# Attention sums queued later, taps respread, and row transfers re-timed in a metaformer layer with routed experts

## The chip, the cores and the metric

One core of a Trainium2 chip runs the whole kernel. The metric is device time in microseconds (us); the median of 3 runs is 2202.95 (2195.85 to 2204.05). All data is fp32.

## The reference, cut to what matters

Four images of 256 channels and 32 x 32 pixels (N = 1024 positions) go through one layer and then through a feed-forward with eight experts. The layer has a selective scan in four channel groups (Mamba), gated 1-D convolutions, an attention with 8 heads over the 1024 positions, a mixing product, a 3x3 convolution per channel, two normalisations and a projection; the feed-forward sends each position to its two best experts.

```
# scan, in each of four groups:
h = dA_t * h + dBu_t;  y_t = sum over states of h * C_t
# attention, 8 heads of 32:
att = softmax(q @ k.T / sqrt(hd));  o = (att @ v) @ outw.T + outb
# then, per image: mix o with the convolutions (fc), normalise, gelu,
# 3x3 convolution per channel, normalise over the image, project
# feed-forward:
gate = top 2 of softmax(x @ Wg + bg)
out += weight_e * (gelu(x @ W1[e] + b1[e]) @ W2[e] + b2[e])   for the two chosen e
```

## The kernel before, in words

The order of the work is written out by hand. Pieces of work are Python generators; `start` puts one into the list `running`, and each `beat` gives every generator in it one step, if its time has come: what a generator yields is the number of beats until its next step. The instructions go to each engine in the order in which they are emitted so, and each engine works through its own queue in that order; semaphores make an instruction wait for its data.

**The scan** is cut into 32 parts (an image, one of four groups, one half of the positions: eight parts an image) of 16 steps. A step is a decay on ACT (L715), an inflow on DVE (L725), the scan itself on DVE (L736), the product with C on Pool (`dA`, L744) and a sum over states on PE (`yp`, L754); a beat follows each step. Beside it run the work of other images: the convolutions of the image before (`g`, `d` at L454 and L459, `qd`, `gp`), normalisation, and the routing of the image before (`dispatch`, from L1779).

**The pauses.** After the fourth part of image b, for b = 1, 2 and 3, the scan pauses. Attention of image b-1 starts, with the mixing product behind it (`joined`); beside it run the end of the scan part (`finish_part`, with `op` at L769 and L773), and as one chain the `local` convolution of image b-1, `around` of image b-2 (the 3x3 convolution: L1305 to L1334), and further pieces. In the last pause, with attention of image 2, that chain ends in `taps_ahead(3)`: it loads image 3's rows (L587), scales them on ACT (L569), adds two shifted products on DVE (L576, four in all for the two channel blocks) and stores them (L581) for the last convolutions. Beats go on until attention has reached its third last step; then the scan resumes while attention ends.

**Attention** (L1101 to L1190) takes 32 key steps: two head groups, two halves of the queries, eight key blocks. Step by step it emits four logits matmuls for the next step (L1123, one for each head of the group, tile `st`) and their four exps on ACT (L1133, tile `e`), then four matmuls with v (L1169, tile `av`). The softmax's sums come from a product with ones: on odd steps DVE adds the e of two steps (L1179, four additions), and `sum_pair` (L1141 to L1145) multiplies the result by ones (L1143). In the kernel before it is emitted after the av of the next step. `end_block` divides (L1147 to L1159).

**The 3x3 convolution** in `around` (from L1319) takes eight taps besides the centre, two DVE operations each (one for each channel block); it yields 1 after each tap.

**Routing** of an image (`dispatch`) finds the two best experts of each position, counts with two matmuls how many positions before it chose the same expert (`places`, L1867 and L1868, from `oh`), works out each position's row, scales the rows, and then sends them out with 16 indirect transfers from Pool into the DRAM buffer `XS` (L1934, each after a small memset of `apart` at L1933). `follow` makes one instruction wait for another.

**The tail.** After the scan, the last convolutions run with expert tiles beside them; then tiles are held, attention of image 3 runs with its `local`, with image 2's routing under way, then the rest of image 3 and the remaining tiles. A tile loads rows (`xs` from `XS`, L2160), transposes them on PE (`xp`, L2218), and multiplies with the weights (`h`, L2259, gelu on ACT; `y`, L2272); `ys` are added into the output buffer by indirect transfers from Pool (L2299). At the end the rows come back and are added to the result (L2324 to L2331).

The emission of `sum_pair`, before:

```
for i in range(4):
    nc.tensor.matmul(accs[0][ts(i, HD)], v8[...], es[i], ...)
if pairs:
    sum_pair()
if kt % 2 == 0:
    first = es
else:
    for i in range(4):
        nc.vector.tensor_tensor(first[i], first[i], es[i], ALU.add)
    pairs.append((kt, accs[1], first))
```

Of the kernel before, what the change touches and what calls it, by code (L numbers as in the profile page):

```python
# [75 lines left out]
def network(  # L76
# [71 lines left out]
    with tc.tile_pool(name="w_conv", bufs=1) as wp, tc.tile_pool(  # L148
# [955 lines left out]
        def attention(b):  # L1104

            v8, qk = QKV.pop(b)
            rows = [  # L1110
                largest(b, g, qk[g][:, 0, :], qk[g][:, 1, :]) if shifted else None
                for g in range(2)
            ]
            yield 1
            steps = [(g, h, kt) for g in range(2) for h in range(2) for kt in range(NK)]

            def logits(g, h, kt):

                q, k = qk[g][:, 0, :], qk[g][:, 1, :]
                sts = [ps(f"st_{b}_{g}_{h}_{kt}_{i}") for i in range(4)]  # L1120
                for i in range(4):
                    r = ts(i, HD)
                    nc.tensor.matmul(  # L1123
                        sts[i], k[r, ts(kt, P)], q[r, half(h)], start=True, stop=not shifted
                    )
                    if shifted:
                        nc.tensor.matmul(
                            sts[i], ones[HD * i : HD * i + 1, :],
                            rows[g][HD * i : HD * i + 1, half(h)], start=False, stop=True,
                        )  # L1130
                es = [a2(f"e_{b}_{g}_{h}_{kt}_{i}") for i in range(4)]
                for i in range(4):
                    nc.scalar.activation(es[i], sts[i], AF.Exp, scale=1.0 / HD**0.5)  # L1133
                return es

            log_exp()
            ahead = logits(*steps[0])
            pairs, accs, ending = [], [None, None], []

            def sum_pair():  # L1140
                kt, acc, es = pairs.pop()  # L1141
                for i in range(4):
                    nc.tensor.matmul(  # L1143
                        acc[ts(i, HD)], ones[:, 0:HD], es[i], start=(kt == 1), stop=(kt == NK - 1)
                    )  # L1145

            def end_block(g, h, values, total):  # L1147

                low, out = a2(f"low_{b}_{g}_{h}"), OT[b][g][:, half(h)]
                at = (2 * b + g) * 2 + h  # L1150
                nc.scalar.activation(low, total, AF.Ln, bias=added)
                if shifted:
                    nc.scalar.activation(low, low, AF.Exp, scale=-1.0)
                else:
                    nc.vector.tensor_reduce(sums[:, 0, at : at + 1], total, AX.X, ALU.max)
                    nc.scalar.activation(
                        low, low, AF.Exp, scale=-1.0, accum_out=sums[:, 1, at : at + 1]
                    )
                nc.vector.tensor_tensor(out, values, low, ALU.mult)  # L1159

            for at, (g, h, kt) in enumerate(steps):
                es = ahead
                if at + 1 < len(steps):
                    ahead = logits(*steps[at + 1])
                if kt == 0:

                    accs = [ps(f"av_{b}_{g}_{h}_{w}") for w in range(2)]
                for i in range(4):
                    nc.tensor.matmul(  # L1169
                        accs[0][ts(i, HD)], v8[:, kt, ts(4 * g + i, HD)], es[i],  # L1170
                        start=(kt == 0), stop=(kt == NK - 1),
                    )
                if pairs:
                    sum_pair()
                if kt % 2 == 0:
                    first = es
                else:
# [3 lines that stand above are left out]
                    if ending:  # L1181
                        end_block(*ending.pop())
                if kt == NK - 1:
                    ending.append((g, h, *accs))
                if at == len(steps) - 3:
                    T["attended", b] = True
                yield 1
            sum_pair()
            yield 1
            end_block(*ending.pop())  # L1190
            yield 1
# [90 lines left out]
        def around(b):  # L1282

            xc = XC.pop(b)
            mv = small.tile([P, NC2, 2], F32, tag="mv", name=f"mv_{b}")
            for c in range(NC2):
                st = small.tile([P, 2, 6], F32, tag="bn", name=f"bn_{b}_{c}", bufs=2)
                for h in range(2):
                    nc.vector.bn_stats(st[:, h, :], xc[:, c, half(h)])
                nc.vector.bn_aggr(mv[:, c, :], st.rearrange("p a b -> p (a b)"))  # L1290
                yield 1
            rs = small.tile([P, NC2, 2], F32, tag="rs", name=f"rs_{b}")
            root(rs[:, :, 0:1], mv[:, :, 1:2], eps5)
            yield 1
            nc.vector.scalar_tensor_tensor(
                rs[:, :, 1:2], mv[:, :, 0:1], -1.0, rs[:, :, 0:1], ALU.mult, ALU.mult
            )
            yield 1
            xi = XC[b] = a8(f"xi_{b}")
            xz = [  # L1300
                act4.tile([P, HH, WW], F32, tag="a4", name=f"xz_{b}_{c}") for c in range(NC2)
            ]
            pace(b, PACE["taps"])
            for c in range(NC2):
                nc.vector.tensor_scalar(  # L1305
                    xz[c].rearrange("p i j -> p (i j)"), xc[:, c, :], rs[:, c, 0:1], rs[:, c, 1:2],
                    ALU.mult, ALU.add,
                )
            for c in range(NC2):
                nc.vector.tensor_scalar(  # L1310
                    xi[:, c, :], xz[c].rearrange("p i j -> p (i j)"), col("dwc_w", 9 * c + 4),
                    col("dwc_b", c), ALU.mult, ALU.add,
                )
            yield 1
            for k in (0, 1, 2, 3, 5, 6, 7, 8):
                (to_i, at_i), (to_j, at_j) = (edge(d - 1) for d in divmod(k, 3))
                for c in range(NC2):
                    acc = xi[:, c, :].rearrange("p (i j) -> p i j", j=WW)
                    nc.vector.scalar_tensor_tensor(  # L1319
                        acc[:, to_i, to_j], xz[c][:, at_i, at_j], col("dwc_w", 9 * c + k),  # L1320
                        acc[:, to_i, to_j], ALU.mult, ALU.add,
                    )
                yield 1

        def sent_off(b):

# [39 lines left out]
            pace(b, PACE["routing"])  # L1366
            for ticks in experts.dispatch(
                b, xr, act8.tile(experts.XR, F32, tag="a8", name=f"XR_{b}"), root,
                log_exp,
            ):  # L1370
                if experts.counted == b:
                    pace(b, PACE["rows"])
                yield ticks
# [166 lines left out]
        with tc.manual_schedule(engines=ALL):  # L1540
# [4 lines left out]
            for b in range(B):  # L1545
                for p in range(PARTS):
# [15 lines left out]
                    if b > 0 and p == PARTS // 2 - 1:  # L1562
                        drain()
                        start(
                            one_by_one(attention(b - 1), joined(b - 1)), finish_part(at),
                            one_by_one(
                                local(b - 1), *([around(b - 2)] if b > 1 else []),
                                *([normalised(b + 1)] if 1 < b < B - 1 else []),
                                *([taps_ahead(b)] if b == B - 1 and b in XD else []),
                            ),  # L1570
                        )
                        if b > 1:
                            flag = "attending" if b == B - 1 else "joining"
                            start(behind_flag((flag, b - 1), sent_off(b - 2)))
                        if b == 1:
                            start(normalised(b + 1))
                        while not T.get(("attended", b - 1)):
                            beat()
                        resume(at + 1)
# [41 lines left out]
class Experts:  # L1621
# [154 lines left out]
    def s1(self, name):  # L1776
        return self.m0.tile([P, self.NT, 1], F32, tag=name, name=name)

    def dispatch(self, b, X1, XR, root, log_exp):  # L1779

        nc, tc, psum, m0, NT = self.nc, self.tc, self.psum, self.m0, self.NT
        s1, s3, all_e = self.s1, self.s3, self.all_e
# [77 lines left out]
        nc.vector.tensor_tensor(oh, oh1, oh2, ALU.add)  # L1860
        ex, w_1 = s1("ex"), s1("w_1")
        nc.vector.tensor_tensor(ex, m_2, m_1, ALU.subtract)
        yield 1
        cp = bank(f"places_{b}")
        flat = oh.rearrange("p t e -> p (t e)")
        W = NT * NE
# [64 lines left out]
        for j in range(2):  # L1931
            for t in range(NT):
# [6 lines left out]
                for other in self.sent + self.read:  # L1939
                    tc.declare_no_dep(ins.ins, other.ins, reason="no two share a row")  # L1940
                self.sent.append(ins)
                if b == self.B - 1 and j == 0:
                    self.blank_end(t)
                yield 2 if b in (0, 2) or b == 1 and t % 2 else 1
# [487 lines left out]
```

## Time and profile before

| | |
|---|---|
| median of the runs | 2202.95 us |
| profiled execution: time / span | 2182.24 us / 2180.3 us |
| mean granted TensorE clock | 0.953 |
| PE busy | 1937.3 us (89%), 8690 matmuls |
| weight loads busy | 874.4 us (40%) |
| DVE busy | 1533.4 us (70%) |
| ACT busy | 1212.4 us (56%) |
| Pool busy | 1048.1 us (48%) |
| key steps of attention, images 0 / 1 / 2 / 3 | 437.0-537.1 / 795.5-897.5 / 1193.0-1292.6 / 1605.9-1688.5 us |
| end of the scan's last product on Pool | 1449.6 us |
| row transfers of images 0 / 1 / 2 / 3, first to last issue | 1033-1100 / 1391-1445 / 1610-1633 / 1846-1870 us |

Times of the trace count from the start of the span. A row of the groups gives line, engine and operation, the output and inputs by name, the shape, the count, then busy time, the mean of one, and the idle time just ahead of it with what ended that. A bracket in the timeline has the idle time of the engine ahead of an instruction and the instruction that released it. A stretch of the program's windows gives the busy time of each engine in it.

### The profile page before, as it was taken

Reading aid. Unit: us, or ns where it says so; the run is one execution under the profiler, and the core shown is the slowest. Engines: PE = TensorE matmul, PEld = TensorE weight load, DVE = VectorE, ACT = ScalarE, POOL = GpSimd, SP = SyncE. Lnnn points to the kernel's source line nnn. Section 1 sums busy time; section 2 is a strip of 40 time slices with the busy share of each in tenths; the row PEclk is TensorE's granted clock in tenths of the full one; section 3 lists DMA queues with packets and bytes.
Section 4 is the critical chain, followed back from the end, with each engine's and each line's share of the span. In section 5 each row is a group of like instructions: output and inputs, shape, how many; then the busy total and the mean of one; then the engine's idle time right before and its main releaser. Section 6 shows DMA issues by size and latency. Waiting matters only on the chain. (4 is left out here: it accounts for less than half of the span.)

```text
span 2180.3 us, 28168 instructions
## 1 busy us (share of the span) xinstructions
PE 1937.3 (89%) x8690; PEld 874.4 (40%) x8690; DVE 1533.4 (70%) x2231; ACT 1212.4 (56%) x2272; POOL 1048.1 (48%) x930
## 2 busy tenths in 40 slices
PE   6778778999978999987789999768999999999995
PEld 2113112322212332222123223225642668888884
DVE  4989998857999988799898888985365356121211
ACT  4665657668668577776566776625168423222221
POOL 0887887712888740476977025752040013422221
PEclk8988999999999999998999999889999999999997
DMA  3565553401444421153634024454230166967665
GB/s 107 146 162 123 127 125 91 106 22 59 116 115 107 111 60 39 34 132 100 177 79 113 1 78 101 104 177 123 78 115 1 46 196 198 261 186 191 175 162 167
DMA packets 157087, 251.40 MB, mean 115 GB/s; under 512 B 34740, under 2 KB 101332, under 8 KB 156664
## 3 DMA queue, kind: packets, MB, share of 16 engines
q1 hardware_dynamic: 136560, 223.47, 37.8%
q0 software_dynamic: 12720, 17.32, 4.0%
q10 hardware_dynamic: 7640, 8.65, 1.2%
q8 instruction: 72, 1.18, 0.2%
q14 instruction: 95, 0.78, 0.1%
HBM read 137.22 MB, written 36.62 MB: 80 GB/s over the span
## 5 line engine op out<-in xcount | busy, mean ns | idle before, releaser
L744 POOL TENSOR_TENSOR dA<-hs,cs 128x512 f32<-128x512 f32 x512 | 683.2, 1342 | 374.8 <-DVE hs L736 315.8
L715 ACT ACTIVATE dA<-dts,A 128x512 f32<-128x512 f32 x512 | 358.7, 718 | 159.2 <-DMA dts<-dt 71.8
L754 PE MATMUL yp<-dA,quads 128*32 128x512 f32 x1024 | 290.0, 640 | 85.3 <-POOL dA L744 74.0
L2299 POOL DMA_INDIRECT Y<-ys,dest x68 | 108.8, 1601 | 507.6 <-DVE ys L2291 500.2
L1133 ACT ACTIVATE e<-st 128x512 f32<-128x512 f32 x512 | 263.8, 605 | 93.2 <-PE st L1123 85.8
L2264 ACT ACTIVATE hs<-h,b 128x256 f32<-128x256 f32 (+1 forms) x256 | 110.5, 478 | 334.7 <-PE h L2259 231.7
L725 DVE TENSOR_TENSOR dBu<-dts,bs 128x512 f32<-128x512 f32 x384 | 260.0, 678 | 49.8 <-PE bs L707 14.8
L736 DVE TENSOR_TENSOR_SCAN hs<-dA,last,dBu 128x512 f32<-128x512 f32 x192 | 243.7, 1269 | 3.3 <-PE yp L754 1.1
L2272 PE MATMUL y<-w,hs 128*128 128x256 f32 (+1 forms) x1088 | 244.6, 384 | 0.0
L2259 PE MATMUL h<-xT,w 128*128 128x256 f32 (+1 forms) x1024 | 237.4, 388 | 0.1
L736 DVE TENSOR_TENSOR_SCAN hs<-dA,dBu 128x512 f32<-128x512 f32 x192 | 232.0, 1208 | 3.7 <-PE av L1143 2.7
L1179 DVE TENSOR_TENSOR e<-e,e 128x512 f32<-128x512 f32 x256 | 170.0, 726 | 76.0 <-ACT e L1133 40.2
L2272 PEld LDWEIGHTS y<-w,hs 128*128 128x128 f32 (+1 forms) x1088 | 199.1, 190 | 36.3 <-issue 8.7
L2259 PEld LDWEIGHTS h<-xT,w 128*128 128x128 f32 x1024 | 194.5, 191 | 43.6 <-issue 11.0
L2222 DVE COPY xT<-xp 128x512 f32<-128x512 f32 (+1 forms) x36 | 23.3, 646 | 245.5 <-PE xp L2218 245.2
L707 PE MATMUL bs<-u,xpwT_s 128*32 128x512 f32 x1024 | 162.8, 652 | 34.9 <-DVE hs L736 15.1
L1123 PE MATMUL st<-qk 32*128 32x512 f32 x1024 | 174.8, 638 | 1.9 <-DVE hs L736 1.9
L754 PEld LDWEIGHTS yp<-dA,quads 128*32 128x32 f32 x1024 | 51.1, 114 | 298.1 <-POOL dA L744 194.1
L1169 PE MATMUL av<-e,v 128*32 128x512 f32 x1024 | 138.6, 604 | 0.0
L1123 PEld LDWEIGHTS st<-qk 32*128 32x128 f32 x1024 | 59.9, 183 | 116.7 <-issue 86.2
L1143 PE MATMUL av<-e,every 128*32 128x512 f32 x512 | 86.8, 594 | 4.1 <-DVE e L1179 4.1
L725 DVE TENSOR_TENSOR bs<-dts,bs 128x512 f32<-128x512 f32 x128 | 86.2, 674 | 0.7 <-DMA dts<-dt 0.7
(335 smaller groups left out, 2625.0 us busy)
## 6 DMA issues: line engine op xcount, KB each, us to landing
dts<-dt SPq DMA_DIRECT2D x512, 128.0 KB, 2.4
w<-in_W_dram SPq DMA_DIRECT2D x124, 512.0 KB, 3.9
cs<-cd SPq DMA_DIRECT2D x512, 64.0 KB, 2.1
xs<-XS SPq DMA_DIRECT2D x32, 260.0 KB, 4.2
xd<-xn SPq DMA_DIRECT2D x64, 128.0 KB, 3.0
xn<-in_x_dram SPq DMA_DIRECT2D x8, 512.0 KB
XL<-xl SPq DMA_DIRECT2D x8, 512.0 KB
xl<-XL SPq DMA_DIRECT2D x4, 1024.0 KB
```

Of the source, the lines that this page charges most:

```text
L707: nc.tensor.matmul(bs[r], xpwT_s[:, n, s : s + 1].to_broadcast([P, 32]), T[b, n, "u"][:, half(h)], start=True, stop=True,)
L715: nc.scalar.activation(dA, T[b, n, h, "dts", g][:, 0, :], AF.Exp, scale=A[:, g, n, q : q + 1])
L725: nc.vector.tensor_tensor(dBu, T[b, n, h, "dts", g][:, 1, :], T[b, n, h, "bs", q], ALU.mult)
L736: nc.vector.tensor_tensor_scan(hs, T[b, n, h, "dA", i], dBu, 0.0 if h == 0 else last, ALU.mult, ALU.add)
L744: nc.gpsimd.tensor_tensor(dA, hs, T[b, n, h, "cs", q], ALU.mult)
L754: nc.tensor.matmul(T[b, n, h, "yp"][ts(g, 32)], quads, T[b, n, h, "dA", q * GD + g], start=False, stop=(q == GS - 1),)
L1123: nc.tensor.matmul(sts[i], k[r, ts(kt, P)], q[r, half(h)], start=True, stop=not shifted)
L1133: nc.scalar.activation(es[i], sts[i], AF.Exp, scale=1.0 / HD**0.5)
L1169: nc.tensor.matmul(accs[0][ts(i, HD)], v8[:, kt, ts(4 * g + i, HD)], es[i], start=(kt == 0), stop=(kt == NK - 1),)
L1179: nc.vector.tensor_tensor(first[i], first[i], es[i], ALU.add)
L2259: nc.tensor.matmul(hp[:, i, :], w1(c, k0 + i), xT[:, c, :], start=(c == 0), stop=(c == NC2 - 1))
L2272: nc.tensor.matmul(yp[ts(k % parts, n), ts(t % 2, C)], hidden(k)[:, ds(t * P, n)], w2(k), start=(k < parts), stop=(k >= NHC - parts),)
```

## The change

1. `sum_pair` is emitted at the head of a key step, ahead of the next logits, on odd steps and in the last six steps, and no longer after the av of the even step.
2. `around` of the second image (b = 1) yields 2 after each tap instead of 1; `taps_ahead(3)` is started at once with the pause instead of standing at the end of the chain of `local`, `around` and `normalised`.
3. `dispatch` yields 4 instead of 1 ahead of the `places` matmuls where other work runs beside it (`beside`: images 0 and 1). All that follows in that routing is emitted three beats later.
4. Each of the 16 row transfers of the third image (b = 2) waits for the exp of attention of image 3 that was emitted last.

```diff
@@ attention
-                    nc.scalar.activation(es[i], sts[i], AF.Exp, scale=1.0 / HD**0.5)
+                    ins = nc.scalar.activation(es[i], sts[i], AF.Exp, scale=1.0 / HD**0.5)
+                T["exps"] = ins if b == B - 1 else None
                 return es
...
             for at, (g, h, kt) in enumerate(steps):
                 es = ahead
+                if pairs and (kt % 2 or at > len(steps) - 6):
+                    sum_pair()
                 if at + 1 < len(steps):
                     ahead = logits(*steps[at + 1])
...
-                if pairs:
-                    sum_pair()
                 if kt % 2 == 0:
                     first = es
@@ around
-                yield 1
+                yield 2 if b == B - 3 else 1
@@ routing
-                log_exp,
+                log_exp, lambda: T.get("exps"),
@@ the pause
                                 *([normalised(b + 1)] if 1 < b < B - 1 else []),
-                                *([taps_ahead(b)] if b == B - 1 and b in XD else []),
                             ),
                         )
+                        if b == B - 1 and b in XD:
+                            start(taps_ahead(b))
@@ dispatch
-        yield 1
+        yield 4 if beside else 1
         cp = bank(f"places_{b}")
...
                 self.sent.append(ins)
+                if b == self.B - 2 and recent():
+                    self.follow(ins, [recent()], "one after the other")
```

More of the change, by code (lines that the diff above doesn't have):

```diff
@@ L1777, in s1, with dispatch @@
         return self.m0.tile([P, self.NT, 1], F32, tag=name, name=name)
-    def dispatch(self, b, X1, XR, root, log_exp):
+    def dispatch(self, b, X1, XR, root, log_exp, recent):
         nc, tc, psum, m0, NT = self.nc, self.tc, self.psum, self.m0, self.NT
```

## The prediction

> **What bounds the kernel now.** I read the slices of the page first, then busy time in chosen stretches, then the waits by engine, then single instructions in the attention loops and at the start of the tail. The slices (each 54.5 us):
>
> ```profile
> PE   6778778999978999987789999768999999999995
> ...
> DVE  4989998857999988799898888985365356121211
> ...
> POOL 0887887712888740476977025752040013422221
> PEclk8988999999999999998999999889999999999997
> ```
>
> Pool falls to 0 to 2 three times before slice 26 and while it does so DVE leaves its nines: these are the pauses, in which the scan stands still and an attention runs (key steps from 437.0 to 537.1, 795.5 to 897.5 and 1193.0 to 1292.6 us, images 0 to 2). The fourth attention runs alone at 1605.9 to 1688.5. The stretches, with the columns PE, PEld, DVE, ACT, POOL busy, clock, DMA share, GB/s:
>
> ```profile
> 200.00:240.00 40.00, 30.07 (x110) 6.04 (x110) 40.00 (x47) 22.25 (x39) 33.24 (x27) 1.00 0.55 129
> 1190.00:1292.00 102.00, 99.69 (x663) 27.59 (x665) 81.39 (x109) 75.39 (x148) 6.34 (x4) 1.00 0.10 30
> 1445.00:1475.00 30.00, 24.37 (x115) 15.36 (x116) 20.18 (x33) 12.87 (x21) 5.91 (x7) 0.83 0.72 247
> 1520.00:2150.00 630.00, 615.35 (x3015) 449.15 (x3013) 219.64 (x597) 222.66 (x447) 144.29 (x168) 0.99 0.51 142
> ```
>
> In the scan DVE is busy 40.00 of 40 us: it is the bound. In the tail PE is (615 of 630). In a pause neither is full: a chain sets it. Each key step goes exps (four on ACT, 2.07) → four av matmuls (0.9) → on every second step four sum matmuls (1.0) → next four logits (1.1) → exps. The exps start every 2.07 and 3.13 us in turn where nothing disturbs: 5.2 us a pair. The sums wait for the pair's adds on DVE:
>
> ```profile
> PEld av L1143 <- DVE e L1179: 26.2, 43, 1.9
> ...
> DVE e L1179 <- ACT e L1133: 40.2, 17, 3.5
> ```
>
> 26.2 us over 43 waits, at most 1.9. One such place, in the third pause:
>
> ```profile
> 1254.44 2.48 DVE L1179 TENSOR_TENSOR e<-e,e 128x512 f32<-128x512 f32 x4
> 1255.17 0.14 PEld L1143 LDWEIGHTS av<-e,every 128*32 128x32 f32 x2 [1.90 <-DVE e L1179]
> ...
> 1256.84 4.66 DVE L1319 SCALAR_TENSOR_TENSOR xi<-xz,V,xi 128x992 f32<-128x992 f32 x4
> ...
> 1259.11 3.15 ACT L1133 ACTIVATE e<-st 128x512 f32<-128x512 f32 x6 [3.84 <-PE st L1123]
> ```
>
> Four taps of the 3x3 (4.66 us) lie between two groups of adds (2.48 each), 7.1 us against a pair of 5.2: adds come late, sums wait, logits stand behind the sums, ACT starves for 3.84.
>
> **What the Trainium skill says.** "TensorE: Matmul & The Clock Gate", section "Architectural detail", puts it that TensorE takes matmuls in order and only weight loads may go ahead; so a sum that waits holds the logits behind it. The trace agrees (1.90 above, with the 3.84 after it). The same page's section on HAM oscillation says that long idle gaps of PE bring a cold clock: the mean clock is 0.74 in 1000 to 1040, where PE idles 6.89 once. "Perfetto Trace Analysis", "Summary: the profiler window per engine type", says that a DMA's movement lies outside its issue's window: a row scatter shows about 1.0 us on Pool, yet lands 2.5 to 3.2 after its issue here. No other page bears on it.
>
> **Part 1, pair sums a step later.** It adds and removes no instruction. Read from the changed kernel's order, attention's own matmuls stay as they were: a sum moves from behind an even step's av to ahead of the next step's logits, between which attention has nothing. Only other tasks' matmuls of that beat (L769, L773, the means at L435) now go ahead. In the loops such matmuls are few (in the 1253 to 1262 stretch none), so the ordinary sums gain 0; were each of the 43 waits filled it would be 26, which I exclude, as PE also lacks work to fill them with. The exception is the last six steps: the sums of keys 26,27 and 28,29 go one logits and av earlier. Good: attention ends sooner, and the resumed scan waits for its end less. Bad: where adds are late, logits now wait. First pause: the adds of 26,27 end at 526.1, so one logits group starts some 2.6 later; its end gains about 1.0 (ACT waited 1.90 there): +1.6. Second pause: ACT waited 3.04 for the last sums at 895.90, and DVE 5.00 at 897.51; I take -2.1, two steps' sums (2×1.0) off the end. Fourth attention: nothing else on DVE, nothing to wait at the end but two sums: ends between -1 and +2.6, I take +1.0. Third pause: in part 2's sum.
>
> **Part 2, second image's taps spread, third image's row taps started early.** It moves 16 DVE operations at L1319 (1.22 each), 4 at L576 (1.28), 2 ACT at L569 (1.25) and SP's loads and stores at L587 and L581. Two taps instead of four now lie between adds: 2.3 + 2.5 = 4.8, under 5.2. In steps 18 to 26 of that loop the starts exceed 5.2 a pair by 7.1 us in all. DVE has idles of 2.99, 0.48 and 0.31 early in the pause (1195 to 1210) into which the four L576 (5.1 us) now fall. What they leave:
>
> ```profile
> 1269.32 1.28 DVE L576 SCALAR_TENSOR_TENSOR taps<-xt,V,taps 128x1023 f32<-128x1023 f32 x1 [3.00 <-ACT taps L569]
> ...
> 1284.11 1.28 DVE L576 SCALAR_TENSOR_TENSOR taps<-xt,V,taps 128x1023 f32<-128x1023 f32 x1 [1.29 <-ACT taps L569]
> ...
> 1292.07 1.22 DVE L736 TENSOR_TENSOR_SCAN hs<-dA,dBu 128x512 f32<-128x512 f32 x1 [1.43 <-PE av L1143]
> ```
>
> Gone are 3.00 and 1.29 on DVE, and on ACT the 1.25 of L569 and 1.71 that it waited for the load of xt (issued 1277.1), ahead of exps. But the taps spread to where the four L576 were, so DVE's work in the pause is the same 81 us of 102; what falls is idle. Following the order through with these durations, the resumed scan's first two hs start 4.4 and 5.8 earlier: I take -5.8. From both sides: -7.1 (all excess) and -1.4 (the 1.43 of the last line, which falls with the earlier sums), -8.5; at the other end 0, if something else delays the adds.
>
> **Part 3, counts product three beats later (images 0 and 1).** Two places matmuls (0.36 each) and all behind them go three ticks (5.3 us) later: PE no longer waits 6.89 at 1015.57 and 3.34 at 1374.57. DVE bounds there and had no idle at that time (38.39 and 39.38 busy of 40), so nothing is gained: 0, ±1. The rest of the routing moves too: ACT's and DVE's scaling of rows, and 16 scatters a routing on Pool (1.0 + 0.1 each). For image 0 they stay amid the scan, Pool being busy 33 of 40 there. For image 1 they reach the scan's end: before, the last scatter is at 1444.85, with three dA (1.28 each) behind it, and it is this that tile 0's row load waits for.
>
> ```profile
> 1444.85 1.02 POOL L1934 DMA_INDIRECT XS<-XR,to  x1 [0.17 <-issue]
> 1445.89 3.70 POOL L744 TENSOR_TENSOR dA<-hs,cs 128x512 f32<-128x512 f32 x3
> ...
> 1450.63 1.08 PE L2218 MATMUL xp<-ident,xs 128*128 128x128 f32 x4 [7.40 <-DMA xs<-XS]
> 1451.64 1.94 PE L754 MATMUL yp<-dA,quads 128*32 128x512 f32 x8
> ```
>
> After: two dA among the last scatters; the last dA ends some 1.3 later (1450.9), the last scatter at about 1452 (1444.85 + 6.2 + 1.0) and the rows land at about 1456.9 (before 1450.5). But in the changed order the twelve yp (0.6 each) and the first op stand ahead of xp, and SP's loads for the last convolutions ahead of the xs. So PE works when dA is done, and z, op, xm, qd and gp run 2 to 5 us sooner; PE has lost nothing by about 1472. Later idles of PE, 4.71 at 1495.73 (rp on DVE's d L459) and 2.50 at 1516.54, belong to that chain and shrink in part. Ends: -5 (those shrink by 2/3) and +6.2 (nothing fills). I take -2.
>
> **Part 4, third image's scatters after an exp each.** Adds a wait per scatter on Pool, queued behind which are only the next scatters (Pool is at 0.00 in 1640 to 1720). Before, the 16 ran in a bunch at 1610 to 1633 with the exps' pace of 2.07 and 3.13 unchanged; so no contention to remove: 0. They now end at about 1690 at the latest, with the attention. Ends: 0 and +2.
>
> **Sum.** +1.6 - 2.1 + 1.0 - 5.8 - 2 + 0 = -7.3. The profiled execution took 2182.24 (span 2180.3 and 1.9 around it): it goes to 2175. It lies 20.7 under the runs' median of 2202.95, so the difference is carried over: 2196.
>
> **Rivals.**
> A, larger gain: all 8.5 of part 2, 3 from the ends of the other attentions, and 5 off the tail's 4.71 + 2.50: -16, or 2187. For: DVE's idle at 897.51 is 5.00; against: the sums' ordinary waits stay.
> B, nothing: attention's gain of 5.8 is met by xs 6.2 later, as the tail is PE-bound and its 7.40 gap grows: 2203. For: 7.40 is a wait for this very load; against: yp and op stand ahead now.
> C, slower: the two early sums in each attention hold logits, as in the first pause: 2.6 each, two in all four is 20.8; less the 5.8 of part 2 it is +15, 2218. It decides from adds of those pairs ending over 1 us after the av ahead of the sum. Against: in the fourth DVE is free.
> D, the change isn't what it says: the order shows ordinary sums no later among attention's matmuls; the forecast has that in it, and part 1 alone would give +0.5, 2203.
>
> **How the numbers follow.** Forecast 0.50 (2193 to 2203), A 0.28, B and D 0.11, C 0.11. A measurement here can tell about 0.5%, 11 us, from no change. Faster by that needs 2192: A and a little of the forecast, 0.34; slower, above 2214: C, 0.10; within: 0.56. The range reaches from 2184 (most of A) to 2209 (B with part 1's +2.6 twice).
>
> **What would show it.** Right: exps of the third pause spaced 5.2 a pair through steps 18 to 26, no DVE wait on L569 there, the pause some 6 shorter; places without PE idle yet DVE as busy; xp at about 1457 less the time gained before; the fourth attention unchanged. Wrong: new waits of st or av L1143 on adds near each attention's end, Pool's scatters holding dA, or the tail's first 30 us with PE idle over 10.

## The result, and the profile after

The changed kernel took 2175.88 us (median of 5 runs, 2173.48 to 2176.83) against 2202.69 for the kernel before: a ratio of 0.988, 95% interval 0.9866 to 0.9895, or 26.8 us faster. The prediction had 2196, some 7 faster. Yet the two profiled executions, 2182.24 before and 2175.20 after, differ by 7.0 only. The first of these is not among the timed runs of its kernel, the second is. So two questions stand: were the steps of the sum right, and what do the timed runs of the kernel before hold that its profile doesn't?

The slices of the page after, the same rows as in the prediction:

```profile
PE   6778778999987999988789999679999999999995
...
DVE  4989999957998989699898998985364445121111
...
POOL 0887887712788850476887026742021113322221
PEclk8888999999999999998999999889999999999997
```

Little shows at this grain. The stretches of the program after, with the columns as before:

```profile
200.00:240.00 40.00, 29.95 (x113) 6.04 (x110) 40.00 (x46) 22.84 (x40) 33.46 (x27) 1.00 0.55 131
1190.00:1292.00 102.00, 101.03 (x686) 27.47 (x685) 88.21 (x118) 81.76 (x159) 7.56 (x6) 1.00 0.16 46
1445.00:1475.00 30.00, 26.18 (x120) 17.69 (x120) 26.28 (x30) 14.64 (x22) 4.63 (x5) 0.94 0.67 220
1520.00:2150.00 630.00, 604.81 (x2980) 442.14 (x2979) 214.10 (x592) 219.55 (x442) 142.67 (x168) 0.99 0.51 143
```

DVE's 81.39 of 102 in the third pause has become 88.21: the same work is done sooner, and more of the scan behind it falls into the window. The waits of the whole program show what part 1 did to ordinary sums:

```profile
DVE e L1180 <- ACT e L1133: 47.8, 17, 4.4
...
PEld av L1144 <- DVE e L1180: 27.6, 47, 1.9
```

27.6 us over 47 waits, where it was 26.2 over 43: the sums wait as long as they did. Now the place in the third pause that the prediction showed:

```profile
1254.04 4.13 ACT L1133 ACTIVATE e<-st 128x512 f32<-128x512 f32 x8 [1.14 <-PE st L1123]
1254.09 2.49 DVE L1180 TENSOR_TENSOR e<-e,e 128x512 f32<-128x512 f32 x4
...
1256.50 2.41 DVE L1320 SCALAR_TENSOR_TENSOR xi<-xz,V,xi 128x992 f32<-128x992 f32 x2
1256.68 0.13 PEld L1144 LDWEIGHTS av<-e,every 128*32 128x32 f32 x4 [0.30 <-DVE e L1180]
...
1259.24 3.15 ACT L1133 ACTIVATE e<-st 128x512 f32<-128x512 f32 x6 [1.07 <-PE st L1123]
```

Two taps (2.41) stand between the adds, the sum waits 0.30 instead of 1.90, and ACT idles 1.07 ahead of its exps, not 3.84: a pair takes 5.2 (from 1254.04 to 1259.24). At the start of the tail PE now shows:

```profile
1443.74 0.59 PE L769 MATMUL op<-xn,skips 128*128 128x512 f32 x1
1444.26 2.11 PE L773 MATMUL op<-z,moutT_s 128*64 128x512 f32 x4
1447.90 0.63 PE L2222 MATMUL xp<-ident,xs 128*128 128x128 f32 x4 [1.54 <-DMA xs<-XS]
...
1452.92 2.78 PE L918 MATMUL qd<-xm,qdwT_s 128*32 128x512 f32 x24
```

The idle ahead of xp is 1.54, not 7.40, as op stands in it.

By stages, from single instructions of both traces (us; "attention" is from the first exp's start to the last one's end; the other rows are from start to start):

| stretch | before | after | predicted change | change |
|---|---|---|---|---|
| first attention | 100.1 | 101.6 | +1.6 | +1.5 |
| second attention | 102.0 | 100.0 | -2.1 | -2.0 |
| resumed scan's first hs, third pause, at | 1286.7 | 1280.9 | -4.4 | -5.8 |
| its second hs, at | 1292.1 | 1284.9 | -5.8 | -7.1 |
| last scan operation on DVE, at | 1444.1 | 1435.4 | -5.8 | -8.7 |
| from there to the fourth attention's first exp | 161.8 | 156.0 | -2 (range -5 to +6.2) | -5.8 |
| fourth attention | 82.6 | 84.1 | +1.0 | +1.5 |
| from its last exp to the last y matmul | 454.4 | 460.0 | 0 | +5.7 |
| span | 2180.3 | 2173.3 | -7.3 | -7.0 |

### The profile page after: what moved, and what is told of

The parts are those of the page before. It is cut to its first block, busy times and chain, and to the rows that moved or that the text cites. A ratio compares the mean times of both kernels' runs of the same rounds, so it can differ in the third digit from the quotient of the medians.

```text
span 2173.3 us, 28179 instructions
## 1 busy us (share of the span) xinstructions
PE 1937.3 (89%) x8690; PEld 867.6 (40%) x8690; DVE 1536.4 (71%) x2231; ACT 1211.4 (56%) x2272; POOL 1042.7 (48%) x930
## 5 line engine op out<-in xcount | busy, mean ns | idle before, releaser
L1936 POOL DMA_INDIRECT XS<-XR,to x64 | 65.4, 1021 | 90.3 <-ACT e L1133 53.9
```

## The experiments

There were 18 runs in five groups; the kernels of a group ran side by side with the kernel before. The kernel before stands at one of two levels, the same throughout a group: 2184.87 and 2182.76 in the first and the fourth group, 2202.16, 2202.80 and 2204.06 in the others. The number of the chip doesn't decide it: the first, third and fourth group all have chip 14 on record.

The traces show the two levels apart in one more way. Those of the first and the fourth group hold 25,073 to 25,096 records of a DMA's completion each; those of the other groups 23,593 to 23,900, whatever the kernel, and what is missing is missing after 1000 us, where the row transfers begin. The trace of the first result's changed kernel (23,774) goes with the upper level, the first one of the kernel before (25,091) with the lower. So the two profiles of the prediction and the result come from different levels by this mark, and in a trace of the upper level a wait without a releaser may be for a completion that was not recorded.

**The kernel before, again** (no edit; first group).

> The kernel before, unchanged. The profiled execution took 2182.24 us, the timed runs about 2202, while after's profile and runs agree (2175.20 and 2175.88). Theory 'a stall in some executions': a fresh profile of before that comes out at 2195 or more shows a stretch of about 20 us that the first one lacks, in the same stages otherwise; I expect it where indirect row transfers are close together (image 2's bunch beside the fourth attention, or image 1's at the scan's end). Rival 'profile and timed runs differ by a constant': the fresh profile gives 2182 again and no stage is longer. Ratio to before: 1.000.

2184.92, ratio 0.9997 (0.998 to 1.0014), span 2187.4. No stretch was 20 us longer; the fourth attention took 82.6. The expected stall was not there, but neither was the time of 2202.

**Part 4 alone**, in the first and in the third group:

```diff
+                T["exps"] = ins if b == B - 1 else None
...
+                if b == self.B - 2 and recent():
+                    self.follow(ins, [recent()], "one after the other")
```

> Part 4 alone: image 2's row transfers each wait for an exp. Theory 'a stall in some executions, by the bunch': the timed runs fall by about 20 us to 2182, the profile stays at 2182. The prediction's reading (nothing to remove): timed runs 2202, 0.0%. Rival 'part 2 carries it': 2202.

2185.93 against 2184.87: 1.0007 (0.9994 to 1.002), nothing. The same edit in the third group:

> Part 4 alone once more. Theory: where the kernel before takes 2202, 2202 - 14 = 2188 (-0.65%); where it takes 2185, no difference, as in the first run of it. Rival 'pacing is worth nothing anywhere': no difference in both.

2187.55 against 2202.80: 0.9938 (0.9921 to 0.9955), 15.2 faster. Pacing is worth nothing at the lower level and 15 at the upper.

The two profiles of this one kernel also show what pacing does not remove. From the fourth attention's last exp on, they agree within 0.1 us for 185 us of expert matmuls. Then, just behind the 16 row transfers of image 3 (to 1867.7), which are not paced, the one at the upper level loses 3.9, with PE idle for 1.34 at 1872.17 and no releaser. To the last y it takes 458.2, against 454.3.

**Part 2 alone, and its halves** (the first in the first group, the halves in the second):

```diff
-                yield 1
+                yield 2 if b == B - 3 else 1        # spread_alone, taps_alone
...
-                                *([taps_ahead(b)] if b == B - 1 and b in XD else []),
+                        if b == B - 1 and b in XD:
+                            start(taps_ahead(b))    # early_alone, taps_alone
```

> Part 2 alone: taps at two beats each and image 3's row taps started at once. The prediction: the resumed scan's hs 4.4 to 5.8 us earlier, timed runs 2196.5 (-0.27%). Rival 'part 2 carries it': -20 or more, 2182 or less, by another stretch than the third pause.

2176.82: 0.9963 (0.9951 to 0.9974), 8.05 faster; the third attention took 91.0 instead of 99.6.

> Half of part 2: two beats between taps of the second image, with image 3's row taps still behind them in the chain (so even later). Theory 'the dense taps cost the time': steps 18 to 26 of the third attention lose 7.1 of excess, but the row taps now fall into the resumed scan, where DVE has no idle: 5.1 us of DVE work back: about -2. Rival 'the spread alone is enough': -7 or more.

2198.45 against 2202.16: 0.9978 (0.9967 to 0.9989), 3.7 faster.

> The other half of part 2: image 3's row taps started at once, the second image's taps as dense as before. Theory: the waits of 3.00 and 1.29 on DVE and those on ACT go, four DVE operations (5.1 us) lie in the early idle: -4. Rival 'the early start carries all of it': -8 or more.

2201.84: 0.999 (0.9979 to 1.0), nothing. My -4 was wrong. The traces say why (us from the third attention's first exp):

| | before | early_alone | spread_alone | taps_alone | after |
|---|---|---|---|---|---|
| to its last exp's end | 99.6 | 99.5 | 91.0 | 91.0 | 92.2 |
| to the last scan operation | 251.2 | 251.1 | 248.9 | 240.6 | 242.4 |

(The kernel before, run again, had 254.6 in the last row, so that differences under 4 of single profiles are not read.) The dense taps alone cost the attention its 8.6 us, whether the row taps come early or not. But with the taps spread and the row taps behind them, these four operations fall into the resumed scan:

```profile
1292.31 1.25 DVE L576 SCALAR_TENSOR_TENSOR taps<-xt,V,taps 128x1023 f32<-128x1023 f32 x1
...
1296.39 1.41 DVE L576 SCALAR_TENSOR_TENSOR taps<-xt,V,taps 128x1023 f32<-128x1023 f32 x1
...
1306.54 1.90 DVE L576 SCALAR_TENSOR_TENSOR taps<-xt,V,taps 128x1023 f32<-128x1023 f32 x1 [0.55 <-ACT taps L569]
...
1311.29 1.25 DVE L576 SCALAR_TENSOR_TENSOR taps<-xt,V,taps 128x1023 f32<-128x1023 f32 x1
```

This is DVE's timeline of spread_alone: 5.8 us of row taps among scan operations, where DVE is the bound. Of the 8.6 that the attention gained, 2.3 are left at the last scan operation. Only both halves together keep it.

**Part 1 alone** (first group):

```diff
+                if pairs and (kt % 2 or at > len(steps) - 6):
+                    sum_pair()
...
-                if pairs:
-                    sum_pair()
```

> Part 1 alone: pair sums at the head of the next odd step, two of them earlier at each end. The prediction: +0.5 us, 2203, with the first attention 1.6 longer, the second 2.1 shorter and the fourth 1.0 longer. Rival 'the early end sums shorten every pause': -4 or more, 2198.

2183.01 against 2184.87: 0.9995 (0.9983 to 1.0006), nothing that can be told. Its attentions took 101.6, 100.0, 98.3 and 84.1: the first, second and fourth as in the changed kernel.

**Part 3 alone** (second group):

```diff
-        yield 1
+        yield 4 if beside else 1
         cp = bank(f"places_{b}")
```

> Part 3 alone. The prediction: scan not shorter, image 1's last row transfer about 6 later, gap of PE ahead of the first xp larger or filled by yp and op, 4.71 and 2.50 later in the tail shrinking: -2 in all. Theory from the profile of after: the fourth attention starts about 7 earlier after the same scan, and some 6 is given back after it: -1 to -2. Rival 'nothing is given back without the other parts': -7.

2200.1 against 2202.16: 0.9989 (0.9979 to 0.9999), 2.1 faster, which the interval barely sets apart from nothing. From the last scan operation to the fourth attention it took 156.0, where kernels without part 3 take 161.8, a gain of 5.8. From that attention's last exp to the last y matmul it took 460.5. The two of the same group without part 3, spread_alone and early_alone, took 456.7 and 457.7 there, so 2.8 to 3.8 of the gain are given back. (Before, again, has 454.3, but at the lower level.)

The profile of places_alone held what the first group had not shown: a fourth attention of 95.8 us. Those of spread_alone and early_alone too: 96.8 and 97.1. Two views of early_alone; first the stretch in question (busy time of PE, PEld, DVE, ACT and Pool, then clock, DMA share and GB/s):

```profile
1606.00:1616.00 10.00, 10.00 (x71) 3.23 (x73) 8.85 (x24) 8.15 (x16) 7.36 (x11) 1.00 0.76 206
1616.00:1626.00 10.00, 5.81 (x23) 1.54 (x20) 3.96 (x5) 1.19 (x2) 8.47 (x17) 0.74 0.30 106
1626.00:1636.00 10.00, 9.08 (x25) 2.07 (x24) 0.83 (x2) 2.65 (x6) 4.88 (x9) 0.75 0.21 75
```

and the same stretch of before_again, whose bunch of transfers began at 1616 instead of 1612:

```profile
1616.00:1626.00 10.00, 10.00 (x80) 2.93 (x80) 9.10 (x13) 8.43 (x17) 8.66 (x16) 1.00 0.48 132
1626.00:1636.00 10.00, 10.00 (x84) 2.55 (x76) 6.71 (x10) 8.22 (x16) 8.66 (x16) 1.00 0.29 104
```

From 1616 to 1626 ACT is busy for 1.19 us of 10 and DVE for 3.96, PE for 5.81, and DVE for 0.83 in the next 10; Pool alone goes on at its pace, sending rows. The timeline of early_alone there:

```profile
1615.77 1.14 PE L1123 MATMUL st<-qk 32*128 32x512 f32 x8
...
1619.32 0.96 POOL L1935 DMA_INDIRECT XS<-XR,to  x1 [0.19 <-issue]
...
1622.46 0.60 ACT L1133 ACTIVATE e<-st 128x512 f32<-128x512 f32 x1 [6.50 <-remote]
...
1623.11 4.19 PE L1123 MATMUL st<-qk 32*128 32x512 f32 x4 [4.14 <-issue]
...
1624.58 0.60 ACT L1133 ACTIVATE e<-st 128x512 f32<-128x512 f32 x1 [1.52 <-remote]
...
1635.17 2.50 DVE L1179 TENSOR_TENSOR e<-e,e 128x512 f32<-128x512 f32 x4 [14.60 <-PE st L1123]
```

An exp whose logits were done at 1616.9 begins at 1622.46, with an idle of 6.50 for which the trace has no releasing instruction of the core ("remote"); PE idles 4.14 with no releaser; then exps and logits go one by one, 2.1 us each, and DVE has waited 14.60. In between the granted clock is one half, from 1620.8 to 1631.0 in the trace's clock records. "TensorE: Matmul & The Clock Gate", section "Part 1: The HAM clock gate", of the Trainium skill has this clock follow from an idle PE. Here it fell 1.8 us after the end of PE's last matmul ahead of the gap (1618.97), and av matmuls took 1.06 each in it and 0.59 outside. So the clock did not begin the stall, as the engines had stopped before it fell; what the slower matmuls add to the stall was not measured.

**Pacing taken away, or made coarser** (third and fifth group):

```diff
-                if b == self.B - 2 and recent():
+                if b == self.B - 2 and recent() and t % 4 == 0:         # quads
+                if b == self.B - 2 and recent() and t == 0:             # eights
+                if b == self.B - 2 and recent() and j == 0 and t == 0:  # bunch_later
...
+        if b == self.B - 2:     # bunch_later, ahead of the loop over transfers
+            yield 10
```

In no_paced the condition and the wait behind it are gone.

> The changed kernel without part 4. Theory 'a bunch of 16 row transfers can stop the fourth attention': on a chip where the kernel before takes 2202, this takes 2178 + 14 = 2192, its fourth attention 97 us from first to last exp instead of 84, with idle of ACT and PE that no instruction of the profile ends, and the clock at half for some 10 us after it. Where before takes 2185: 2176, the attention 84. Rival 'the other parts together remove the stall': 2178 on either.

2186.32 against 2202.80: 0.993 (0.9908 to 0.9951); the fourth attention took 96.5 and the clock was at half for 10.2 us, as expected. The time was not: 2192 had been expected.

> The changed kernel with only each fourth row transfer of image 2 waiting for an exp, so four bunches of four instead of sixteen singles. Theory 'the stall begins when more than a few are on their way' (in the stalled profiles it begins 4 to 6 us after the start of the bunch, after some 4 transfers): no stall, 2178, attention 84. Rival 'any back-to-back transfers stall': +14 on a chip where before takes 2202. On one where it takes 2185 nothing is told apart.

2177.93: 0.9903 (0.9883 to 0.9923), attention 84.3. Bunches of four cost nothing that can be told.

> The changed kernel with the bunch kept (only the first transfer waits for an exp), but ten beats later, away from the weight and row loads at the attention's start. Theory 'the bunch by itself stops the engines': the stall of some 14 us appears later in the attention, 2192 where before takes 2202. Rival 'it takes the bunch and the loads of the tiles together' (512 KB of weights and 260 KB of rows are issued within 5 us of it): no stall, 2178.

2187.75: 0.9934 (0.9914 to 0.9954). The bunch ran from 1620 to 1642, and key steps 13 to 16 took 2.57, 4.38, 2.49 and 5.62 where the changed kernel has 2.07 and 3.13 in turn: the stall moves with the bunch, away from the loads at the attention's start. In this one profile it was shorter (attention 88.7) and the clock was not halved, though the runs lost as much; so whether the loads add to the stall at the start is left open.

> The changed kernel without part 4 once more. Theory: 2176 where before takes 2183 to 2185, the fourth attention 84 us; 2186 where it takes 2202. Rival 'pacing costs or gains with no regard to the level': 2186 in both.

At the upper level again: 2186.43 against 2204.06, 0.992 (0.9905 to 0.9935), attention 97.1. Whether the bunch costs nothing at the lower level, in company with the other parts, was not seen.

> The changed kernel with only each eighth row transfer of image 2 waiting for an exp: two bunches of eight. Bunches of four gave 2177.9, one of sixteen 2186 to 2188, where before takes 2203. Theory 'it needs more than some five transfers on their way': two bunches of eight stall as well, 2182 or more, the attention 88 to 97 us long. Rival 'only the long bunch stalls': 2178, 84 us.

This group was at the lower level: 2178.31 against 2182.76, 0.9977 (0.9966 to 0.9989), attention 84.1. It tells nothing of bunches of eight. But with all four parts in it, it is the nearest to the changed kernel at this level: 4.5 faster.

**The changed kernel, again** (no edit; second and fifth group).

> The changed kernel, unchanged. The first comparison gave 2175.9 against 2202.7 (-27), yet the two profiles differ by 7.0, and the kernel before took 2184.9 in the second set of runs. Theory 'two levels of the kernel before': with runs on one chip side by side, the change is worth what the profiles show plus the scatter of the scan, -7 to -11 (2174 to 2178 where before is 2185). Rival 'the 27 is real': 2158 where before is 2185, ratio 0.988.

2177.57 against 2202.16: 0.9876 (0.9852 to 0.99). The rival was right on the ratio, and wrong on where it would hold.

> The changed kernel, unchanged. In the two groups of runs in which the kernel before took 2202 it took 2176 and 2178. Theory: it is the same 2176 to 2178 where the kernel before takes 2183 to 2185, so the change is worth -7 there (-0.3%) and -25 elsewhere (-1.1%), and the difference is the stall. Rival 'chip time varies as a whole': 2158 where before takes 2184, ratio 0.988 again.

2178.10 against 2204.06: 0.9884 (0.9867 to 0.9901), at the upper level once more. So the changed kernel itself was never timed beside the kernel before at the lower level. What stands for it there are eights and the kernels that lack one part of it:

**One of the other parts taken away** (fourth group; before 2182.76). Each is the changed kernel with the hunks of one part undone, as in the diffs above.

> The changed kernel without part 2. Alone that part gave -8.0. Theory 'the parts add up apart from the stall': 2178 + 8 = 2186 where before takes 2202 (2183 where it takes 2185), with DVE waits on L569 of 3.0 and 1.3 back in the third attention. Rival 'part 1's earlier end sums do the same work': 2180.

2180.75: 0.9994 (0.998 to 1.0009), between the 2183 expected and the rival's 2180.

> The changed kernel without part 3. Alone it gave -2.4. Theory 'its gain in the tail is given back after the fourth attention': 2178 + 2 = 2180, while the fourth attention starts some 7 later relative to the scan's end. Rival 'the tail's order of PE work is worth all of its 7': 2185.

2175.93: 0.9972 (0.9962 to 0.9982), with 161.8 us from the last scan operation to the fourth attention and 455.3 from that one's last exp to the last y (the other three of the group: 459.0 to 459.2).

> The changed kernel without part 1. Alone it gave -1 with an interval that holds 0. Prediction: 2177 to 2178, no difference; with the fourth attention at 82.6 instead of 84.0. Rival 'with the taps spread, the earlier end sums matter': 2182 or more.

2176.19: 0.9971 (0.9959 to 0.9984), fourth attention 82.6. Without the taps hardly a gain is left; without part 1 or part 3 it is 6.6 and 6.8, no less than the 4.5 of eights. The taps are the part that counts at the lower level; parts 1 and 3 show no gain there.

## Why the prediction was wrong, and where it was right

**Part 4 is the step that failed.** The prediction said of the 16 transfers: "so no contention to remove: 0", because the exps kept their pace in the profile of before. That was true of the execution shown, which by its records belongs to the lower level, and not of the runs, which were at the upper. Every profile of an unpaced kernel taken in a group with before at 2202 or more stalls (places_alone, spread_alone, early_alone, no_paced twice at 95.8 to 97.1, bunch_later at 88.7); none of the three from the first group does, nor the first profile of before (82.6; 84.1 with part 1). The two levels of before lie 17.3 to 21.3 apart. The stall is 12.5 to 14.5 us of that in the full-length ones, and from its last exp to the last y the kernels without part 3 lose another 2.4 to 3.9, most of it behind image 3's transfers; that the transfers cause it was not tried. Pacing alone is worth 15.2 at the upper level, so the term that was 0 should have been -15 there. With pacing in place, the other parts add 9.6 (2187.55 to 2177.93), not far from the 7.3 forecast for them. Counted in the other order, they are worth 16.5 and pacing 8.4: the split depends on the order, but in neither is pacing 0.

**The second failing is in the sum's last step:** "so the difference is carried over". The 20.7 between the profiled execution and the runs of the same kernel was taken as an offset that the changed kernel would have too. It was a cost that the profile had escaped, as a profile of one level stood beside runs of the other; the changed kernel's profile and runs agree (2175.20 and 2175.88). The 20.7 could be read off the table before the prediction.

**Part 2** was right in its mechanism: sums 0.30 late at the place shown, a wait of 0.57 for L569 in place of those of 3.00 and 1.29, the row taps in DVE's early idle. Its size was set too low: the two hs came 5.8 and 7.1 earlier and not 4.4 and 5.8, the last scan operation 8.7, and the part alone is worth 8.05. Its bound of -8.5 held in these runs (interval 5.7 to 10.7); in the profile of taps_alone the last scan operation comes 10.6 sooner after the attention's start.

**Part 1**: +1.5, -2.0 and +1.5 stand against +1.6, -2.1 and +1.0. The predicted sum of +0.5 is nothing that runs can tell, and so is the measured one. Ordinary sums gained nothing, as the waits above show. That logits wait for sums placed early (rival C) is so in the first and the fourth attention, at 1.5 each and not 5.2, and in the third, which takes 92.2 in the changed kernel and 91.0 in no_sums.

**Part 3** was net right and half seen. The idle ahead of xp was filled by op, as worked out, and xp came at 1447.90, which with the 8.7 gained before is the 1457 that was forecast. The tail to the fourth attention shrank by 5.8, more than the -2 taken. Not foreseen was the other half: 2.8 to 3.9 lost behind that attention, against kernels of the same group without part 3. (The 5.7 of the table compares a lower-level profile with an upper-level one.) The net is 1.9 to 3.0 in the profiles and 2.1 in the runs of places_alone. One reading of this part was too narrow: the 2.5 to 3.2 us in which a scatter lands are the shortest and the median, the longest took 7.2. Of after's waits of PE between 1675 and 1890:

```profile
PE xp L2222 <- DMA xs<-XS: 3.6, 1, 3.6
PE mean L435 <- DVE xi L1320: 2.9, 1, 2.9
PE places L1869 <- DVE oh L1862: 2.1, 1, 2.1
```

where before had 4.2 for the first and neither 2.9 nor 2.1 for the others. no_places has 0.8 and none, so these waits come with part 3, but for 0.8; by which reordering of tiles was not tried.

**Rival A** named -16 and thought of the attention's ends and the tail; the sum is nearer to it, the reason is another. Rival B's tail did not eat the gain, as yp and op stood ahead.

**What stays open.** Why the kernel before keeps to one level through a group of runs, and what in the chip stops ACT and PE. As every stalled trace lacks completion records, the recording itself may have a part in the stall; whether all timed runs were recorded is not known, and a run without recording was not made. Another candidate can be argued against: "Runtime: NRT & Kernel Launch", section "Instruction fetch mechanics", of the Trainium skill has instructions come in by DMA in pages of 16 KiB; the page of that stretch was fetched 9.7 us after the attention's first exp in early_alone and 9.6 in before_again, taking 1.44 and 1.53 us, so it was not late. In bunch_later it came after 9.4, and attention went on at its pace for 21 us more. How long a bunch between 4 and 16 transfers must be for the stall is not known. And the gains do not add up: -15.2 for pacing alone and -16.5 for the rest alone give -31.7, together it is -24.9 (quads) or -24.6. In company pacing is worth 8.4 in the runs, though it removes 12.5 in the profile. Six runs of no_paced from 2181 to 2193 may mean that not each of them stalls as long; that is not shown.

## What to carry to other kernels

Where a profiled execution lies well below the timed runs of the same kernel, the difference is a finding, not an offset. Here a stage cost more in the runs than in the profile, and it was one whose transfers come in a burst. Indirect transfers issued back to back beside a tight chain are worth spreading even where one profile shows them free; a wait at each fourth was enough here. Work taken out of a pause is only gained if it doesn't land where its engine is the bound. A gain in one stretch of a long tail is to be followed to the end of the tail before it is counted, and compared with kernels of the same group of runs.

## What the runs showed that was not expected

- Beside a bunch of 16 indirect row transfers (one each 1.26 us) attention on PE, ACT and DVE came nearly to a stand for some 10 us while Pool went on, in each of the five traces of the upper level that have the bunch at the attention's start; the clock was at half for 10.2 us then (in spread_alone twice for 6.8).
- The same kernel, with the same chip number on record, kept to 2185 in one group of runs and to 2203 in another, and the traces of the second kind lack 5 to 6% of the completion records.
- Four operations of 1.25 to 1.90 us that fell from a pause into the resumed scan cost 6.3 of the 8.6 us that the pause had gained.
